# Row maxima of attention scores: from a relu of key differences to one maximum over two PSUM banks, with the keys in two groups of rows

## The chip, the cores and the metric

The kernel runs on one core of a Trainium2 chip. The metric is the device time of one execution in microseconds. The engines are TensorE (PE in the profile: matmuls; PEld: its weight loads), VectorE (DVE), ScalarE (ACT), GpSimd (POOL) and SyncE (SP), which here issues most DMAs. Each engine works through its own list of instructions in order. They meet at semaphores.

## The reference

An attention block with a gated bias by relative position, then a layer of eight experts. Shapes: 8 batches, 1024 tokens, 256 features, 16 heads of 16.

```python
q, k, v = split_heads(x @ Wq.T + bq), split_heads(x @ Wk.T + bk), split_heads(x @ Wv.T + bv)
pos_bias = transpose(rel_embed[buckets], (2, 0, 1))        # head, query, key
proj = (split_heads(x) @ gru_W.T + gru_b).reshape(B, H, N, 2, 4).sum(-1)
gate_a, gate_b = split(sigmoid(proj))
gate_out = gate_a * (gate_b * gru_const - 1.0) + 2.0
scores = einsum('bhid,bhjd->bhij', q, k) * scale + gate_out * pos_bias
attn = softmax(scores, axis=-1)
x = layernorm(x + (einsum('bhij,bhjd->bhid', attn, v) merged) @ Wo.T + bo)
# then: top 2 of 8 experts per token with a capacity, a fallback network for what spills
x = layernorm(x + experts(x))
```

## The kernel before, in words

The attention part works in units: one batch and two heads, 64 units in all. A unit has 16 steps. In the loop over `g`, step `s` of unit `u` stands for one block of 128 keys (`j`) and one half of the 1024 queries (`c`, 512 of them), for both heads. `scores` forms the transposed scores: two bf16 matmuls into the two banks of `sc`, of which there are two copies. `exps` adds the gated near bias (`gb`, made on GpSimd by `gate_biases`) on VectorE where the block has near keys, and takes the exponential of 128x1024 on ScalarE. On the odd steps `products` multiplies the exponentials with the values: four matmuls with 17 columns each, side by side, into `o_acc`. Queries and keys are held as three bf16 parts; `PRODUCTS` names the six pairs of parts that are stacked along the contraction, 16 rows each. Behind these 96 rows lie 24 rows for the far bias and two for the shift.

The exponential needs the largest score of each query first. That maximum is formed 21 steps (`LEAD`) ahead, one block of 128 queries and one head per step `m = g + LEAD`. The 1024 keys are split in two halves of each block of 128 keys. `max_first(m)` forms the scores of the difference between the first and the second half's keys (`KD`, in `ks_d`), with the difference of their biases, in the bank `pm1`; ScalarE's relu of it goes to `over`. `max_second(m)` forms the scores of the second half in the bank `pm0`, or on some even steps in the bank that the other streams share. `max_fold(m)` adds the two and takes the maximum over 512 columns in one VectorE instruction, since max(a, b) is b + relu(a - b). Each half takes two matmuls (`half_scores`): keys against queries (512 columns), and the near bias by a diagonal matrix of gates (`dgb`, from `diagonal` on GpSimd; 192 to 320 columns). Once a unit has its 16 maxima, `shift` transposes them and stores them as two rows of `QS`.

The order is written out by hand. Beside the steps run streams, Python generators that are moved on once per step: the next batch's projections (`prologue`, `halves`, `gating`), the last batch's output projection and expert choice (`epilogue`), and per unit `shift` and `divide`. Where a stream yields BANK, `streams.bank` lets it issue a matmul into the one shared bank (pool `ps_x`); where it yields HELD or SLOW, the read of that bank follows at the start of the next step, on ScalarE or VectorE (`streams.held`). Within a step the order is: `max_fold` of the maximum before, `held`, `scores`, `max_first`, `exps`, products, `bank`, `max_second`. If an even step's held read was SLOW (`behind`), `bank` follows `max_second`.

[...]four for `sc`, two for `pm0` and `pm1`, one shared, one for `o_acc`.

The operands of a unit are loaded by `load_unit` on SP's queue, two units ahead, at steps 3 (keys), 4 (differences) and 6 (queries), six or seven DMAs each, into `KS`, `KD` and `QS`. On the same queue are the bias windows (step 1 and 8), the gates (9 and 15), the sums of the exponentials and their reciprocals (steps 2 to 5, which `divide` needs at step 8), the outputs, and the streams' loads and stores.

After the attention the experts follow (from about 2600 us on); the change does not touch them.

Of the kernel before, what the change touches and what calls it, by code (L numbers as in the profile page):

```python
# [42 lines left out]
R_FAR, R_SHIFT, R_ALL = 6 * D, 6 * D + 24, 6 * D + 26  # L43
HP = 2
# [34 lines left out]
def tile_attention_moe(  # L79
# [73 lines left out]
    with ExitStack() as at:  # L153
# [16 lines left out]
        def bank(name):  # L170
            pool, tag = banks[0]
            banks.append(banks.pop(0))
            return pool.tile([P, CH], F32, tag=tag, name=name)
# [145 lines left out]
        for lo, hi in zip(cuts[:-1], cuts[1:]):  # L319
# [18 lines left out]
        nc.vector.tensor_tensor(  # L338
            strip16[:, 1, : STRIP - HALF], strip[:, : STRIP - HALF], strip[:, HALF:],
            ALU.subtract,  # L340
        )
# [17 lines left out]
        dd = [dram.tile([3, E, N // 2], BF16, name=f"dd{i}") for i in range(2)]  # L359
# [11 lines left out]
        QS = [cst.tile([R_ALL, HP, N], BF16, name=f"qs{i}") for i in range(3)]  # L371
        KS = [cst.tile([R_ALL, HP, N], BF16, name=f"ks{i}") for i in range(3)]
        KD = [cst.tile([R_SHIFT, HP, N // 2], BF16, name=f"ks_d{i}") for i in range(2)]
        pattern = once.tile([R_ALL, HP, N], F32, tag="oD", name="pattern")
        for h in range(HP):
            for part in range(3):
                r = R_FAR + part * NI
                nc.sync.dma_start(out=pattern[r : r + NI, h, :], in_=kcr[:NI, :])
            for r in range(R_SHIFT, R_ALL):
                nc.sync.dma_start(out=pattern[r : r + 1, h, :], in_=kcr[8:9, :])  # L380
        for t in KS:
            nc.gpsimd.tensor_copy(t[R_FAR:], pattern[R_FAR:])
        for t in KD:
            nc.gpsimd.memset(t[R_FAR:], 0.0)
# [26 lines left out]
        def first_part(n, parts, rest):  # L411
            after(n, lambda: nc.scalar.copy(parts[:, 0, :], rest))
            after(n + 1, lambda: nc.gpsimd.tensor_tensor(
                rest, rest, parts[:, 0, :], ALU.subtract
            ))

# [9 lines left out]


        def first_parts(parts, rest):
            nc.scalar.copy(parts[:, 0, :], rest)
            nc.gpsimd.tensor_tensor(rest, rest, parts[:, 0, :], ALU.subtract)  # L430

        def last_parts(parts, rest):
            nc.scalar.copy(parts[:, 1, :], rest)
            nc.gpsimd.tensor_tensor(parts[:, 2, :], rest, parts[:, 1, :], ALU.subtract)
# [174 lines left out]
        def halves(b, xT, m):  # L609
# [3 lines left out]
            for c in range(NCH):  # L613
                for w_sb, b_sb, dst in ((wk_sb, bk_sb, kd), (wq_sb, bq_sb, qd)):
# [14 lines left out]
                    pv = pq.rearrange("p (j a n) -> p j a n", a=2, n=HALF)  # L629
                    if dst is kd:  # L630

                        second = rt.tile([P, CH // 2], F32, tag="second", name="second")
                        sv = second.rearrange("p (j n) -> p j n", n=HALF)
                        nc.scalar.activation(
                            sv, pv[:, :, 1, :], AF.Identity, bias=bias, scale=1.0
                        )
# [9 lines left out]
                    if dst is kd:  # L646
                        dif = rt.tile([P, CH // 2], F32, tag="dif", name="dif")
                        dparts = work.tile(
                            [P, 3, CH // 2], BF16, tag="dparts", name="dparts"
                        )  # L650
                        nc.vector.scalar_tensor_tensor(
                            dif.rearrange("p (j n) -> p j n", n=HALF),
                            pv[:, :, 0, :], bias, sv, ALU.add, ALU.subtract,
                        )
                        first_part(1, dparts, dif)
                        second_part(3, dparts, dif)
                        after(5, lambda t=dparts, c=c: nc.sync.dma_start(
                            out=dd[b % 2][
                                :, ms, c * (CH // 2) : (c + 1) * (CH // 2)
                            ].rearrange("a r n -> r a n"),  # L660
                            in_=t,
                        ))
# [238 lines left out]
        def load_unit(u, which):  # L901

            b, hp = divmod(u, UB)
            assert batches[b].gated and batches[b].rows >= (hp + 1) * HP * D
            heads = slice(hp * HP * D, (hp + 1) * HP * D)
            if which == 2:
                nc.sync.dma_start(
                    out=QS[u % 3][R_FAR:R_SHIFT],
                    in_=fd[b % 2][:, :, hp * HP : (hp + 1) * HP, :].rearrange(
                        "a j h n -> (a j) h n"  # L910
                    ),
                )
            src, dst = ((kd, KS[u % 3]), (dd, KD[u % 2]), (qd, QS[u % 3]))[which]
            for r, parts in enumerate(PRODUCTS):
                nc.sync.dma_start(
                    out=dst[r * D : (r + 1) * D],
                    in_=src[b % 2][parts[which != 2], heads, :].rearrange(
                        "(h d) n -> d h n", d=D
                    ),
                )  # L920

# [89 lines left out]


        def half_scores(m, a, pm):
            u, n = divmod(m, STEPS)
            i, h = divmod(n, HP)
            me = units[u]
            lo, hi = max(i - NEAR, 0), min(i + NEAR + 1, NI)
            pm = pm.rearrange("p (j n) -> p j n", n=HALF)
            if a:
                keys = KD[u % 2][:, h, :].rearrange("p (j n) -> p j n", n=HALF)  # L1020
            else:
                keys = KS[u % 3][:R_SHIFT, h, :].rearrange("p (j n) -> p j n", n=P)[:, :, HALF:]
            nc.tensor.matmul(  # L1023
                pm, QS[u % 3][:R_SHIFT, h, i * P : (i + 1) * P], keys, start=True, stop=False
            )
            at = (h * 2 + a) * MWIN + (lo - i + NEAR) * P
            nc.tensor.matmul(  # L1027
                pm[:, lo:hi, :],
                dgb[m - h][:, h, :],
                me.biasb[:, at : at + (hi - lo) * P].rearrange("p (j n) -> p j n", n=P)[  # L1030
                    :, :, :HALF
                ],
                start=False,
                stop=True,
            )

        def max_first(m):

            u, n = divmod(m, STEPS)
            me = units[u]  # L1040
            ahead = m + 6
            if m == 0:
                for a in range(0, 6, 2):
                    dgb[a] = diagonal(0, a // 2)
            if ahead % 2 == 0 and ahead < UNITS * STEPS:
                dgb[ahead] = diagonal(ahead // STEPS, ahead % STEPS // HP)
            if n == 0:
                me.mh = rt.tile([P, HP, NI], F32, tag="mh", name=f"mh{u}", bufs=2)
            me.over = rt.tile([P, CH], F32, tag="over", name="over", bufs=2)
            pm = ps_m.tile([P, CH], F32, tag="pm1", name="pm1")  # L1050
            half_scores(m, 1, pm)
            nc.scalar.activation(me.over, pm, AF.Relu)  # L1052

        def max_second(m, common=False):

            pm = bank("pm") if common else ps_m.tile([P, CH], F32, tag="pm0", name="pm0")
            half_scores(m, 0, pm)
            units[m // STEPS].rest = pm

        def max_fold(m):  # L1060
            u, n = divmod(m, STEPS)
            i, h = divmod(n, HP)
            me = units[u]
            nc.vector.tensor_tensor_reduce(  # L1064
                out=me.over,
                in0=me.rest,
                in1=me.over,
                scale=1.0,
                scalar=-3.0e38,
                op0=ALU.add,  # L1070
                op1=ALU.max,
                accum_out=me.mh[:, h, i : i + 1],
            )

        def shift(u):
# [14 lines left out]
            def store():  # L1090
                for a in range(2):
                    nc.sync.dma_start(
                        out=QS[u % 3][R_SHIFT + a : R_SHIFT + a + 1].rearrange(
# [8 lines left out]
        def scores(u, j, c):  # L1102
            me = units[u]
            qs, ks = QS[u % 3], KS[u % 3]
# [159 lines left out]
        for u in range(2):  # L1264
            for which in range(3):
                load_unit(u, which)
            load_max_bias(u)
            clear_max_bias(u)
# [3 lines left out]
        for m in range(LEAD):  # L1272
# [6 lines left out]
            max_first(m)  # L1279
            streams.free()  # L1280
            streams.bank()
            max_second(m)
# [26 lines left out]
        for g in range(G + 12):  # L1309
# [4 lines left out]
            if g < G:  # L1314
# [7 lines left out]
                if u + 2 < UNITS:  # L1322
                    for which, at_ in enumerate((3, 4, 6)):
# [6 lines left out]
                if u + 1 < UNITS:  # L1330
                    if s == 8:
                        load_bias(u + 1)
# [6 lines left out]
            if g < G:  # L1339
                scores(u, j, c)  # L1340
                if m < G:
                    max_first(m)
# [16 lines left out]
            if m < G and g < G:  # L1359
                max_second(m, c == 0 and not behind and not streams.holder)  # L1360
# [10 lines left out]
        banks += [(ps_m, "pm0"), (ps_m, "pm1")]  # L1371
# [264 lines left out]
```

## Time and profile before

| | |
|---|---|
| median of 3 runs | 3706.02 us (3704.2 to 3713.74) |
| the profiled execution | 3705.5 us, of which its span 3703.8 us |
| granted TensorE clock over the span | 0.954 |
| exponentials of the attention loop | from 149.5 to 2523.6 us |
| busy from 1000 to 2000 us | PE 932.2, DVE 627.9, ACT 741.7, POOL 778.4 us |

In the rows of a profile, a group has its line, engine and operation, what it writes and reads, its count, then its busy time in us, the mean in ns, and how long its engine was idle just before it, with what ended most of that. In a timeline a row has its start in us, its duration in us, engine, line and operation, and a count where equal neighbours are merged. Matmuls overlap in the array, so the distance from one start to the next tells more than the duration.

### The profile page before, as it was taken

How to read it: one execution, taken by the hardware profiler on the slowest of the kernel's cores; microseconds unless marked ns; L12 is line 12 of the kernel's file. 1: busy time of each engine (PE TensorE's matmuls, PEld its weight loads, DVE VectorE, ACT ScalarE, POOL GpSimd, SP SyncE). 2: the span in 40 equal slices, each digit the busy share in tenths (PEclk: the TensorE clock that was granted, in tenths of full speed). 3: DMA queues.
4: the chain of work that ended last, by engine and by line, in shares of the span. 5: the costliest groups of instructions: out<-in, count | busy, mean ns of one | idle time of the engine just before them, and what ended most of it. 6: DMA issues, size and time to landing. Idle time of an engine off the chain costs nothing. (4 is left out here: it accounts for less than half of the span.)

```text
span 3703.8 us, 53431 instructions
## 1 busy us (share of the span) xinstructions
PE 3293.6 (89%) x16263; PEld 1663.7 (45%) x16263; DVE 1944.0 (52%) x5559; ACT 2045.0 (55%) x3084; POOL 2221.0 (60%) x2619
## 2 busy tenths in 40 slices
PE   4798898999899999999999999995299999999998
PEld 2242243334334334334333433332176667677776
DVE  2455566665756656665666576662033444344443
ACT  1576776777767777777777777772022222222222
POOL 2566666876886787787787688683333333333332
PEclk8899999999999999999999999996599999999999
DMA  5566666565543444444434444430322321332220
GB/s 133 153 167 192 167 172 183 173 195 181 179 140 110 144 135 122 134 136 122 139 123 141 133 123 128 129 111 15 107 70 74 90 87 54 92 94 94 71 89 22
DMA packets 380594, 455.71 MB, mean 123 GB/s; under 512 B 87653, under 2 KB 285410, under 8 KB 380282
## 3 DMA queue, kind: packets, MB, share of 16 engines
q1 hardware_dynamic: 338602, 388.06, 35.5%
q0 software_dynamic: 19296, 43.38, 4.1%
q10 hardware_dynamic: 22384, 20.58, 1.9%
q8 instruction: 138, 2.26, 0.3%
q14 instruction: 174, 1.43, 0.1%
HBM read 315.16 MB, written 140.54 MB: 123 GB/s over the span
## 5 line engine op out<-in xcount | busy, mean ns | idle before, releaser
L1129 ACT ACTIVATE pr<-sc 128x1024 f32<-128x1024 f32 x1024 | 1046.8, 1023 | 303.7 <-DVE sc L1122 297.9
L983 POOL TENSOR_TENSOR gb<-bias,gates 128x1024 f32<-128x1024 f32 (+2 forms) x512 | 1070.5, 2091 | 190.1 <-DMA gates<-gd 114.3
L1064 DVE CUSTOM_DVE_ANT_0 over<-pm,over 128x512 f32<-128x512 f32 x1024 | 704.3, 688 | 884.7 <-ACT over L1052 281.3
L1052 ACT ACTIVATE over<-pm 128x512 f32<-128x512 f32 x1024 | 609.3, 595 | 344.0 <-PE pm L1027 327.2
L1107 PE MATMUL sc<-qs,ks 122*128 122x512 bf16 x2048 | 625.1, 386 | 26.3 <-ACT pr L1129 18.5
L1122 DVE TENSOR_TENSOR sc<-sc,gb 128x640 f32<-128x640 f32 (+3 forms) x768 | 599.6, 781 | 46.6 <-POOL gb L983 21.0
L1027 PE MATMUL pm<-biasb,dgb 128*128 128x320 bf16 (+2 forms) x2048 | 581.7, 284 | 17.2 <-POOL dgb L996 17.2
L1137 PE MATMUL o_acc<-pr,v 128*17 128x512 f32 x4096 | 562.5, 621 | 0.3 <-ACT pr L1129 0.3
L1474 PE MATMUL ph<-xsT,w 128*128 128x512 f32 (+1 forms) x1440 | 487.6, 497 | 13.0 <-ACT xsT L1414 13.0
L1489 PE MATMUL py<-w,hT 128*128 128x256 f32 x2208 | 485.0, 379 | 5.9 <-DVE ys L1496 5.9
L1489 PEld LDWEIGHTS py<-w,hT 128*128 128x128 f32 x2208 | 419.2, 190 | 74.5 <-issue 10.5
L1023 PE MATMUL pm<-ks,qs 120*128 120x512 bf16 x1024 | 397.8, 388 | 57.3 <-DVE mh L1064 33.9
L1023 PE MATMUL pm<-ks_d,qs 120*128 120x512 bf16 x1024 | 397.1, 388 | 25.0 <-ACT over L1052 13.6
L1023 PEld LDWEIGHTS <-qs 120*128 120x128 bf16 x2048 | 208.9, 102 | 467.4 <-issue 303.4
L1481 ACT ACTIVATE hT<-ph,b_sb 128x512 f32<-128x512 f32 (+1 forms) x360 | 211.6, 588 | 287.3 <-PE ph L1474 286.3
L1474 PEld LDWEIGHTS ph<-xsT,w 128*128 128x128 f32 x1440 | 270.2, 190 | 212.7 <-issue 166.5
L1414 ACT COPY xsT<-pt 128x512 f32<-128x512 f32 (+1 forms) x90 | 39.5, 489 | 566.9 <-PE pt L1411 472.8
L143 POOL TENSOR_TENSOR rs<-rstd,neghalf 128x1 f32<-128x1 f32 x138 | 78.2, 566 | 442.2 <-DVE rstd L141 441.8
L1027 PEld LDWEIGHTS <-dgb 128*128 128x128 bf16 x2048 | 202.4, 99 | 301.6 <-issue 161.8
L996 POOL TENSOR_TENSOR dgb<-anti,grev 128x256 bf16<-128x256 f32 x512 | 314.2, 614 | 4.6
L1107 PEld LDWEIGHTS <-ks 122*128 122x128 bf16 x2048 | 199.8, 100 | 202.0 <-issue 52.3
L419 POOL TENSOR_TENSOR parts<-rest,parts 128x512 bf16<-128x512 f32 (+1 forms) x80 | 92.6, 1158 | 267.0 <-ACT parts L418 201.6
(184 smaller groups left out, 2929.7 us busy)
## 6 DMA issues: line engine op xcount, KB each, us to landing
gates<-gd SPq DMA_DIRECT2D x64, 832.0 KB
biasb<-stripb SPq DMA_DIRECT2D x128, 288.0 KB
gates<-gd SPq DMA_DIRECT2D x64, 576.0 KB
bias<-blocks SPq DMA_DIRECT2D x64, 512.0 KB
xd<-zero SPq DMA_DIRECT2D x51, 522.0 KB
ks<-kd SPq DMA_DIRECT2D x384, 64.0 KB
qs<-qd SPq DMA_DIRECT2D x384, 64.0 KB
yd<-zero SPq DMA_DIRECT2D x40, 512.0 KB
```

Source lines behind the costliest of these rows:

```text
L983: nc.gpsimd.tensor_tensor(gb_[:, :, off : off + hi - lo], me.bias[:, :, off : off + hi - lo], gates[:, :, lo - at : hi - at], ALU.mult,)
L996: nc.gpsimd.tensor_tensor(dg, anti.unsqueeze(1).to_broadcast([P, HP, P]), batches[b].grev[:, i, hp * HP : (hp + 1) * HP] .unsqueeze(2) .to ...
L1023: nc.tensor.matmul(pm, QS[u % 3][:R_SHIFT, h, i * P : (i + 1) * P], keys, start=True, stop=False)
L1027: nc.tensor.matmul(pm[:, lo:hi, :], dgb[m - h][:, h, :], me.biasb[:, at : at + (hi - lo) * P].rearrange("p (j n) -> p j n", n=P)[:, :, :HALF],
L1052: nc.scalar.activation(me.over, pm, AF.Relu)
L1064: nc.vector.tensor_tensor_reduce(out=me.over, in0=me.rest, in1=me.over, scale=1.0, scalar=-3.0e38, op0=ALU.add, op1=ALU.max, accum_out=me. ...
L1107: nc.tensor.matmul(me.sc[:, h, :], ks[:, h, j * P : (j + 1) * P], qs[:, h, c * CH : (c + 1) * CH], start=True, stop=True,)
L1122: nc.vector.tensor_tensor(sc[:, :, lo - c * CH : hi - c * CH], sc[:, :, lo - c * CH : hi - c * CH], me.gb[j][:, :, off : off + hi - lo], A ...
L1129: nc.scalar.activation(pr, sc, AF.Exp)
L1137: nc.tensor.matmul(o_acc[r : r + D + 1, :], batches[b].v[:, j, hp * HP + h, :], prs[c][:, h, :], start=(j == 0), stop=(j == NI - 1),)
L1474: nc.tensor.matmul(ph[:, :size], w1_sb[:, k, f * P : (f + 1) * P], xsT[:, k, :size], start=(k == 0), stop=(k == NK - 1),)
L1489: nc.tensor.matmul(py, hT[:, f, t * P : (t + 1) * P], w2_sb[:, f, :], start=(f == 0), stop=(f == NF - 1),)
```

## The change

Differences of keys, their parts and the store `dd` go, and so do the relu and `over`. The maxima get operands of their own, `QM` and `KM`, with three products of parts (`M_PRODUCTS`) instead of six: 48 rows, and 16 rows for two parts of the far bias, make 64. Rows 0 to 63 hold the second half of each block of keys, rows 64 to 127 the first half; the queries are there twice. `maxima(m)` takes the place of `max_first` and `max_second`: two key matmuls of 64 rows each, one on each group of rows, into the two banks of one tile `pm`, then the two bias matmuls. It stands where `max_second` stood. `max_fold` is one maximum over the 1024 columns of both banks. The second bias strip is now that of the first half itself, no longer a difference. `load_unit` has four parts; the operands of the scores are held for two units instead of three and loaded one unit ahead, those of the maxima two units ahead.

```diff
+M_PRODUCTS = PRODUCTS[:2] + PRODUCTS[3:4]
+M_FAR = 3 * D
...
-        QS = [cst.tile([R_ALL, HP, N], BF16, name=f"qs{i}") for i in range(3)]
-        KS = [cst.tile([R_ALL, HP, N], BF16, name=f"ks{i}") for i in range(3)]
-        KD = [cst.tile([R_SHIFT, HP, N // 2], BF16, name=f"ks_d{i}") for i in range(2)]
+        QS = [cst.tile([R_ALL, HP, N], BF16, name=f"qs{i}") for i in range(2)]
+        KS = [cst.tile([R_ALL, HP, N], BF16, name=f"ks{i}") for i in range(2)]
+
+        QM = [cst.tile([P, HP, N], BF16, name=f"qm{i}") for i in range(2)]
+        KM = [cst.tile([P, HP, N // 2], BF16, name=f"km{i}") for i in range(2)]
...
+            if which == 0:
+                for r, (_, part) in enumerate(PRODUCTS):
+                    rows(KS[u % 2], r * D, kd, part)
+            elif which == 1:
...
+                for r, (part, _) in enumerate(PRODUCTS):
+                    rows(QS[u % 2], r * D, qd, part)
+            elif which == 2:
+                for r, (_, part) in enumerate(M_PRODUCTS):
+                    for a, base in ((1, 0), (0, 64)):
+                        for h in range(HP):
+                            head = hp * HP + h
+                            nc.sync.dma_start(
+                                out=KM[u % 2][
+                                    base + r * D : base + (r + 1) * D, h, :
+                                ].rearrange("d (j n) -> d j n", n=HALF),
+                                in_=kd[b % 2][part, head * D : (head + 1) * D, :].rearrange(
+                                    "d (j a n) -> d j a n", a=2, n=HALF
+                                )[:, :, a, :],
+                            )
+            else:
+                for base in (0, 64):
+                    nc.sync.dma_start(
+                        out=QM[u % 2][base + M_FAR : base + 64],
+                        in_=far[:2].rearrange("a j h n -> (a j) h n"),
+                    )
+                    for r, (part, _) in enumerate(M_PRODUCTS):
+                        rows(QM[u % 2], base + r * D, qd, part)
...
-            me.over = rt.tile([P, CH], F32, tag="over", name="over", bufs=2)
-            pm = ps_m.tile([P, CH], F32, tag="pm1", name="pm1")
-            half_scores(m, 1, pm)
-            nc.scalar.activation(me.over, pm, AF.Relu)
...
-            pm = bank("pm") if common else ps_m.tile([P, CH], F32, tag="pm0", name="pm0")
-            half_scores(m, 0, pm)
-            units[m // STEPS].rest = pm
+            me.pm = ps_m.tile([P, 2, CH], F32, tag="pm", name="pm")
+            lo, hi = max(i - NEAR, 0), min(i + NEAR + 1, NI)
+            for a in range(2):
+                rows = slice(a * 64, a * 64 + 64)
+                nc.tensor.matmul(
+                    me.pm[:, a, :], QM[u % 2][rows, h, i * P : (i + 1) * P],
+                    KM[u % 2][rows, h, :], start=True, stop=False,
+                )
+            for a in range(2):
+                at = (h * 2 + a) * MWIN + (lo - i + NEAR) * P
+                nc.tensor.matmul(
+                    me.pm[:, a, :].rearrange("p (j n) -> p j n", n=HALF)[:, lo:hi, :],
+                    dgb[m - h][:, h, :],
...
-            nc.vector.tensor_tensor_reduce(
-                out=me.over,
-                in0=me.rest,
-                in1=me.over,
...
+            nc.vector.tensor_reduce(
+                me.mh[:, h, i : i + 1], me.pm.rearrange("p a n -> p (a n)"), AX.X, ALU.max
             )
...
-                    for which, at_ in enumerate((3, 4, 6)):
+                    for which, at_ in ((2, 4), (3, 7)):
                         if s == at_:
                             load_unit(u + 2, which)
...
+                    for which, at_ in ((0, 3), (1, 6)):
+                        if s == at_:
+                            load_unit(u + 1, which)
...
                 scores(u, j, c)
-                if m < G:
-                    max_first(m)
                 exps(u, j, c)
...
             if m < G and g < G:
-                max_second(m, c == 0 and not behind and not streams.holder)
+                maxima(m)
...
-        banks += [(ps_m, "pm0"), (ps_m, "pm1")]
+        banks += [(ps_s, "sc"), (ps_s, "sc")]
```

## The prediction, made before the changed kernel ran

> **What bounds the kernel now.** I read the page first: which engine is full, and in which part of the span.
>
> ```profile
> span 3703.8 us, 53431 instructions
> PE 3293.6 (89%) x16263; PEld 1663.7 (45%) x16263; DVE 1944.0 (52%) x5559; ACT 2045.0 (55%) x3084; POOL 2221.0 (60%) x2619
> L1064 DVE CUSTOM_DVE_ANT_0 over<-pm,over 128x512 f32<-128x512 f32 x1024 | 704.3, 688 | 884.7 <-ACT over L1052 281.3
> L1052 ACT ACTIVATE over<-pm 128x512 f32<-128x512 f32 x1024 | 609.3, 595 | 344.0 <-PE pm L1027 327.2
> L1122 DVE TENSOR_TENSOR sc<-sc,gb 128x640 f32<-128x640 f32 (+3 forms) x768 | 599.6, 781 | 46.6 <-POOL gb L983 21.0
> L1023 PE MATMUL pm<-ks,qs 120*128 120x512 bf16 x1024 | 397.8, 388 | 57.3 <-DVE mh L1064 33.9
> ```
>
> TensorE is the fullest, and the attention loop (exponentials from 149.5 to 2523.6 us) is where the change lies: 1024 steps, about 2.33 us each. VectorE (0.63 busy between 1000 and 2000 us) and ScalarE (0.74) have room. ScalarE's 609 us of relu are therefore no time of the kernel by themselves: between 1000 and 2000 us TensorE waits on the relu for 5.4 us only.
>
> A busy TensorE is not one at its peak, so I read its timeline next, for the distance from start to start. Two steps, an even one (from 1013.81) and an odd one (from 1015.16):
>
> ```profile
> 1013.81 0.60 PE L1107 MATMUL sc<-qs,ks 122*128 122x512 bf16 x2
> 1014.24 0.38 PE L1023 MATMUL pm<-ks_d,qs 120*128 120x512 bf16 x1
> 1014.46 0.25 PE L1027 MATMUL pm<-biasb,dgb 128*128 128x192 bf16 x1
> 1014.86 0.38 PE L1023 MATMUL pm<-ks,qs 120*128 120x512 bf16 x1
> 1015.07 0.25 PE L1027 MATMUL pm<-biasb,dgb 128*128 128x192 bf16 x1
> 1015.16 0.60 PE L1107 MATMUL sc<-qs,ks 122*128 122x512 bf16 x2
> 1015.59 0.38 PE L1023 MATMUL pm<-ks_d,qs 120*128 120x512 bf16 x1
> 1015.81 0.25 PE L1027 MATMUL pm<-biasb,dgb 128*128 128x192 bf16 x1
> 1015.99 1.05 PE L1137 MATMUL o_acc<-pr,v 128*17 128x512 f32 x8
> 1016.97 0.28 PE L1078 MATMUL pmr<-ident,mh 128*16 128x128 f32 x1
> 1017.08 0.38 PE L1023 MATMUL pm<-ks,qs 120*128 120x512 bf16 x1
> 1017.30 0.25 PE L1027 MATMUL pm<-biasb,dgb 128*128 128x192 bf16 x1
> 1017.39 0.60 PE L1107 MATMUL sc<-qs,ks 122*128 122x512 bf16 x2
> ```
>
> A 512-column bf16 matmul costs 0.215 us in a row of them, not 0.38; a bias matmul 0.09 to 0.14. I cut the PE rows between 1000 and 2000 us at every start of a scores pair: 429 steps, in four classes. Even steps without another stream's matmul: 141, mean 1.34 us. Odd ones without: 103, 2.49 (median 2.28; the products cost about 1.0). Even ones with stream work: 74, 2.90. Odd ones with: 111, 3.05. Weighted, 2.33 us. All but the first class are filled by TensorE's own work.
>
> Third, the stretch before the loop, where maxima run without scores. It shows what a chain "matmul, fold, same bank again" costs:
>
> ```profile
> 137.62 0.38 PE L1023 MATMUL pm<-ks,qs 120*128 120x512 bf16 x1 [0.57 <-DVE mh L1064]
> 137.83 0.27 PE L1027 MATMUL pm<-biasb,dgb 128*128 128x256 bf16 x1
> 138.25 0.69 DVE L1064 CUSTOM_DVE_ANT_0 over<-pm,over 128x512 f32<-128x512 f32 x1
> 139.00 0.38 PE L1023 MATMUL pm<-ks,qs 120*128 120x512 bf16 x1 [0.59 <-DVE mh L1064]
> ```
>
> 137.62 to 139.00 is 1.38 us: 0.21 keys, 0.27 bias, 0.15 to the fold, 0.69 fold, 0.06 back. In the main loop this chain is slack: the even step may take the shared bank for one half and the relu frees the other early.
>
> **The change, part by part.**
>
> *Fold.* One VectorE maximum over 1024 PSUM columns replaces 512 (0.69 us). The trace has no such instruction. Nearest row: the bias add L1122, also on PSUM, takes 293, 559, 827 and 1090 ns for 128, 384, 640 and 896 elements, that is 0.16 us plus 1.04 ns an element: 1.22 us for 1024. Bounds: 0.69 if it read two elements at a time, 1.35 if dearer by a tenth. I take 1.22, which is +0.53 on the chain (VectorE goes from about 1.48 to 1.92 us a step, not full by itself).
>
> *Single buffer.* Both halves are now one two-bank tile with one copy. The four matmuls of m+1 stand behind the fold of m, in TensorE's queue ahead of the next scores. So every step has a floor: keys together 0.22, switch 0.10, first bias 0.11, last bias with its end 0.27, to the fold 0.13, fold 1.22, back 0.06 = 2.11 us. During the 1.41 us of fold and hand-overs TensorE has only two scores (0.43) in an even step without stream work. Such steps go from 1.34 to 2.11, +0.77 us, and 32.9% of the 1003 loop steps that have maxima are such: 330, **+254 us**. Even steps whose only stream work is an expert count (13 of 429, mean 1.59, so 30) go to 2.11 too: **+15**. Before the loop the floor of 1.38 becomes 2.11 in some 13 of 20 folds: **+9**.
>
> *Row groups.* Of the two key matmuls one should disappear beside the other, -0.215 us, in steps that TensorE fills: 1003 - 330 - 30 = 643, which is -138 us. Against this stands a rule of the Trainium skill, "TensorEngine Tiling (Array Packing)", Key Properties: changing the tiling mode, not only the tile, drains the array. The row: the products use 17-column tiles, and at 1015.81 a bias matmul of 192 columns is through after 0.09 (as 1015.07 to 1015.16), yet the products start only after 0.18. A switch costs some 0.09 us; I use 0.10. Each step now switches twice more, into row groups and back. By the page's "up to 2x" alone the filled steps bring -138; with two switches of 0.10 they bring 643 x (-0.215 + 0.20) = **-10**. I take the second. That row groups run together no run here shows (column groups do: eight product records in 0.98 us); bounds of the overlap 0 and 0.215.
>
> *Relu gone.* ScalarE -0.595 us a step; it bounds nothing. TensorE's waits on relu and exponentials are 5.4 and 3.0 us in 1000: **-10** over the loop at most.
>
> *Held reads.* A stream's VectorE read stands behind the fold, so 0.53 later, and the one shared bank is free later. About 22 of 128 steps have such a read and a new bank matmul; 180 steps at 0 to 0.53, say 0.25: **+45**. This wait also holds the maxima behind that matmul.
>
> *SP's queue.* A unit's loads go from 19 DMAs to 33: keys 6, queries 7, maxima's keys 12, maxima's queries 8. At 0.46 us each (six in 2.75) that is +6.4 us of SP a unit. Twelve instead of six stand before the four reciprocals, which so land 2.8 later; TensorE's matmul on them waited 24.7 us in 1000 already. The maxima's queries come last: from the sums at step 2 on, 2.4 + 2.9 + 5.5 + 2.4 + 3.3 + 3.7 and some 2 to land = 22 us, and they are needed at step 11, 9.4 steps later: 21.9 us at 2.33 a step, 24.6 at 2.62. Longer steps cover it, except with a batch's gate stores (16 more DMAs) in between. Bounds 0 and 150; I take **+15**. The 128-byte runs (1536 a unit) at the present mean of 62 ns a packet are 6 us of 16 engines a unit, under the free half of them.
>
> *At nothing:* differences of keys (12 subtractions of 675 ns in 1000 us on POOL, 12 casts and copies on ScalarE), covered because neither engine bounds; uncovered they would be worth -40 us in all. *Moved:* the loads for the scores come one unit ahead instead of two, at steps 3 and 6 of the unit before; they are needed 10 steps (23 us) later, which covers them. The diagonal matrices on POOL are issued behind the exponentials of a step instead of ahead of them, six maxima before their use. TensorE loads as many weights as before. Setup: a few memsets and copies on POOL, 0 to +5. Tail and experts unchanged.
>
> Sum: 254 + 15 + 9 - 10 - 10 + 45 + 15 = +318 us. On the profiled execution's 3705.5 (span 3703.8; median of the runs 3706.0) this gives 4023; I say **4025 us**, a loop of about 2.65 us a step.
>
> **The rivals.**
>
> *Faster (0.05).* TensorE's savings win. It needs a cheap fold: a step's floor is 0.89 plus the fold. Without any switch cost the filled steps give 138 us, and 330 even steps may lose 0.42 each: the fold would have to end within 0.87 us. At 0.69 and no switches the floor is 1.48, the loss 46, and the time about 3706 - 138 + 46 = 3615. For it: the filled classes are two thirds of the steps. Against: the slope of L1122.
>
> *Cheap chain (0.08).* The fold as computed, but switches cost nothing: floor 2.01, 330 x 0.67 = 221, -138, with the small terms +40: about 3830.
>
> *No overlap (0.12).* The row groups run one after the other: +0.215 in all 1003 steps, 4025 + 216 = 4240. The change would then not do what it says.
>
> *SP late (0.10).* Some 2.4 us of stall per unit at step 11: 64 x 2.4 = 155, 4180.
>
> **How the numbers follow.** The chain as summed: 0.65, own range 3920 to 4130. The 80% range reaches to half of the cheap chain and to the late queue: 3860 to 4200; it leaves out most of "no overlap", "faster" and some of "cheap chain". Differences under 0.3% (11 us), about what a measurement of this kernel can tell, get 0.01; slower 0.94.
>
> **What would show it.** Right: on the page, PE's busy share in the loop falls; the maximum takes about 1.22 us; the key matmuls now wait on mh for several hundred us; even steps without stream work take 2.1 us; the first key matmul of a pair and the second start within 0.02 us; 0.1 us gaps around them. Wrong: a maximum under 0.9 us, even steps under 1.7 us, key matmuls 0.2 us apart, or waits of the key matmuls on DMA (qm) that add up to more than 100 us.

## The result, and the profile after

The changed kernel takes 4201.86 us (median of four, 4201.02 to 4204.63), the kernel before 3708.02: a ratio of 1.1331 (95% interval 1.1314 to 1.1348), or 494 us more. Forecast were 319 us more, with 4200 as the end of the range. The chain of matmul and fold was there, in the size computed; of two terms beside it, one was about nine times too small and one about twice.

From the page of the profile after, the rows that answer to those of before:

```profile
span 4202.8 us, 50578 instructions
PE 3347.5 (80%) x16263; PEld 1585.0 (38%) x16263; DVE 2444.5 (58%) x4503; ACT 1495.8 (36%) x1964; POOL 2184.7 (52%) x2558
...
L1051 DVE TENSOR_REDUCE mh<-pm 128x1 f32<-128x1024 f32 x1024 | 1249.1, 1220 | 904.9 <-PE pm L1037 894.4
L1109 ACT ACTIVATE pr<-sc 128x1024 f32<-128x1024 f32 x1024 | 1033.6, 1022 | 1594.1 <-DVE sc L1102 1556.3
...
L1031 PE MATMUL pm<-km,qm 64*128 64x512 bf16 x2048 | 432.1, 403 | 383.5 <-DVE mh L1051 368.7
...
L1157 PE MATMUL pb<-recs,sel 4*128 4x512 f32 x128 | 107.4, 931 | 177.9 <-DMA recs<-sums 163.5
```

The maximum takes 1220 ns, as the slope of the bias adds had said. The key matmuls wait 369 us on it (before: 34). Neither VectorE nor TensorE is full: they wait for each other, VectorE 894 us for the maxima's last matmul, TensorE 369 us for the fold. The last row is the one that was not forecast at its size. TensorE's waits for the reciprocals (us in total, times, longest), before and after:

```profile
PE pb L1177 <- DMA recs<-sums: 74.6, 29, 8.3
```

```profile
PE pb L1157 <- DMA recs<-sums: 163.5, 46, 8.3
```

The mean duration of that matmul rises from 666 to 931 ns.

The timeline of the changed kernel, one even step without stream work:

```profile
1506.32 0.60 PE L1087 MATMUL sc<-qs,ks 122*128 122x512 bf16 x2
1506.53 1.23 DVE L1051 TENSOR_REDUCE mh<-pm 128x1 f32<-128x1024 f32 x1
1507.80 0.39 PE L1031 MATMUL pm<-km,qm 64*128 64x512 bf16 x2 [0.88 <-DVE mh L1051]
1508.13 0.45 PE L1037 MATMUL pm<-biasb,dgb 128*128 128x320 bf16 x2
1508.41 0.60 PE L1087 MATMUL sc<-qs,ks 122*128 122x512 bf16 x2
```

From scores to scores 2.09 us, where an even step took 1.35: scores, fold, maxima, one after the other, with TensorE idle for 0.88. The two key matmuls run together (they start 0.005 us apart in the median of all pairs, and take 0.39 us as a pair, the duration of one). The first bias matmul starts 0.33 us after the first of them: 0.22, the distance of one 512-column matmul before, for both, and about 0.1 that is put down to leaving the row groups.

Cut at every start of a scores pair, as in the prediction, but over the whole loop (from 150 us on), the steps give this table. A class holds mean us, and the sum in us; "reciprocals" are the steps with the matmul that divides by the sums (step 8 of a unit, or soon after), and "early" and "reads" are two experiments below.

| class (count) | before | after | early | early, reads |
|---|---|---|---|---|
| even, no stream work (350 to 352) | 1.33, 464 | 2.05, 722 | 2.06, 726 | 2.04, 717 |
| even, reciprocals (50) | 3.85, 193 | 6.49, 324 | 2.35, 117 | 2.38, 119 |
| even, other streams (111) | 2.54, 282 | 2.91, 323 | 2.94, 327 | 2.83, 314 |
| odd, no stream work (251) | 2.47, 620 | 2.36, 594 | 2.53, 634 | 2.49, 626 |
| odd, stream work (246) | 3.09, 759 | 3.41, 840 | 3.43, 845 | 3.21, 789 |
| odd, reciprocals (13) | 4.10, 53 | 3.98, 52 | 3.97, 52 | 3.15, 41 |

From before to after the first row is +258 us; the second +131, for 50 steps; the third and the fifth, with other streams' work, +41 and +81; the fourth -26.

The second row is SP's queue, on which the reciprocals are loaded. Its timeline, first before, then after, from a unit's sums to its reciprocals:

```profile
1064.65 2.44 SPq L1154 DMA_DIRECT2D sums<-osb  x4
1067.19 2.86 SPq L915 DMA_DIRECT2D ks<-kd  x6
1070.09 2.76 SPq L915 DMA_DIRECT2D ks_d<-dd  x6
1072.94 2.44 SPq L1164 DMA_DIRECT2D recs<-sums  x4
```

```profile
1510.96 2.44 SPq L1134 DMA_DIRECT2D sums<-osb  x4
1513.51 2.86 SPq L887 DMA_DIRECT2D ks<-kd  x6
1516.41 7.64 SPq L907 DMA_DIRECT2D km<-kd  x12
1524.14 2.44 SPq L1144 DMA_DIRECT2D recs<-sums  x4
```

Twelve loads of the maxima's keys take 7.6 us of SP, 0.64 each; the six of the differences took 0.46 each. The reciprocals start 13.2 us after the sums, not 8.3. What that does on TensorE, in another unit of the changed kernel:

```profile
1069.50 0.60 PE L1087 MATMUL sc<-qs,ks 122*128 122x512 bf16 x2
1073.17 2.04 PE L1157 MATMUL pb<-recs,sel 4*128 4x512 f32 x2 [3.07 <-DMA recs<-sums]
...
1075.14 0.61 PE L1031 MATMUL pm<-km,qm 64*128 64x512 bf16 x2
1075.68 0.61 PE L1037 MATMUL pm<-biasb,dgb 128*128 128x256 bf16 x2
1076.09 1.06 PE L1087 MATMUL sc<-qs,ks 122*128 122x512 bf16 x2
```

A wait of 3.07 us, and behind it the array runs at half its rate: 1.06 us for a scores pair that took 0.60. The trace has a granted clock of 0.50 from 1072.9 to 1079.7 us, and 1.00 around that. Over the loop (160 to 2970 us) the granted clock is 0.92, before 0.97.

### The profile page after: what moved, and what is told of

Same layout as the page of the kernel before. It is cut to its first block, busy times and chain, and to the rows that moved or that the text cites. A ratio compares the mean times of both kernels' runs of the same rounds, so it can differ in the third digit from the quotient of the medians.

```text
span 4202.8 us, 50578 instructions
## 1 busy us (share of the span) xinstructions
PE 3347.5 (80%) x16263; PEld 1585.0 (38%) x16263; DVE 2444.5 (58%) x4503; ACT 1495.8 (36%) x1964; POOL 2184.7 (52%) x2558
## 5 line engine op out<-in xcount | busy, mean ns | idle before, releaser
L1051 DVE TENSOR_REDUCE mh<-pm 128x1 f32<-128x1024 f32 x1024 | 1249.1, 1220 | 904.9 <-PE pm L1037 894.4
L1109 ACT ACTIVATE pr<-sc 128x1024 f32<-128x1024 f32 x1024 | 1033.6, 1022 | 1594.1 <-DVE sc L1102 1556.3
L1031 PE MATMUL pm<-km,qm 64*128 64x512 bf16 x2048 | 432.1, 403 | 383.5 <-DVE mh L1051 368.7
L1087 PE MATMUL sc<-qs,ks 122*128 122x512 bf16 x2048 | 650.7, 400 | 11.9 <-ACT pr L1109 6.8
L1117 PE MATMUL o_acc<-pr,v 128*17 128x512 f32 x4096 | 596.5, 656 | 0.3 <-ACT pr L1109 0.3
L1031 PEld LDWEIGHTS <-qm 64*128 64x128 bf16 x2048 | 145.4, 93 | 928.2 <-issue 913.0
L1037 PE MATMUL pm<-biasb,dgb 128*128 128x320 bf16 (+2 forms) x2048 | 432.5, 295 | 23.6 <-POOL dgb L998 23.6
L1157 PE MATMUL pb<-recs,sel 4*128 4x512 f32 x128 | 107.4, 931 | 177.9 <-DMA recs<-sums 163.5
L1489 POOL DMA_INDIRECT out_dram<-o,dst_i x138 | 144.9, 1050 | 160.2 <-DVE o L148 66.9
L1037 PEld LDWEIGHTS <-dgb 128*128 128x128 bf16 x2048 | 117.6, 98 | 275.6 <-issue 236.8
```

Source lines behind the costliest of these rows:

```text
L1031: nc.tensor.matmul(me.pm[:, a, :], QM[u % 2][rows, h, i * P : (i + 1) * P], KM[u % 2][rows, h, :], start=True, stop=False,)
L1037: nc.tensor.matmul(me.pm[:, a, :].rearrange("p (j n) -> p j n", n=HALF)[:, lo:hi, :], dgb[m - h][:, h, :], me.biasb[:, at : at + (hi - lo) ...
L1051: nc.vector.tensor_reduce(me.mh[:, h, i : i + 1], me.pm.rearrange("p a n -> p (a n)"), AX.X, ALU.max)
L1087: nc.tensor.matmul(me.sc[:, h, :], ks[:, h, j * P : (j + 1) * P], qs[:, h, c * CH : (c + 1) * CH], start=True, stop=True,)
L1109: nc.scalar.activation(pr, sc, AF.Exp)
L1117: nc.tensor.matmul(o_acc[r : r + D + 1, :], batches[b].v[:, j, hp * HP + h, :], prs[c][:, h, :], start=(j == 0), stop=(j == NI - 1),)
```

## Experiments

The ratios are to the kernel before on the same chip; the changed kernel stands at 1.1331.

**The keys' loads behind the reciprocals.**

```diff
-                    for which, at_ in ((2, 4), (3, 7)):
+                    for which, at_ in ((2, 6), (3, 7)):
```

> The changed kernel with one number changed: the twelve loads of the maxima's keys are issued at step 6 instead of step 4, and so behind the four loads of the reciprocals. Nothing else moves: maxima's queries still come last. Theory A (TensorE stalls at the reciprocals' matmul because twelve loads of 0.64 us stand ahead of the reciprocals on SP's queue; the clock drops after each stall): the reciprocals are issued about 7.7 us earlier in a unit, waits of that matmul on its data fall from 230 us to under 40, even steps with it from 6.5 us to about 3, granted clock over the loop from 0.92 to 0.96 or more; time about 4000 (3960 to 4040). Rival B (the 128-byte runs load the DMA engines, and the order does not matter): within 40 us of 4202. Rival C (the stall only moves to step 11, since the maxima's queries are as late as before): waits on qm of over 100 us, time 4120 or more.

4242.19 us, 1.1387 (1.136 to 1.1414). Theory A fell as a forecast of the time, and its first half came true: even steps with the reciprocals' matmul fall from 6.49 to 2.32 us. The time went to the next use, as rival C had it: odd steps with other streams' work grow from 840 us of sum to 1041. TensorE's waits by what they wait for:

```profile
PE pm L1031 <- DVE mh L1051: 360.4, 429, 1.6
PE pm L1031 <- DMA qm<-qd: 161.6, 82, 4.8
```

In the changed kernel the maxima's key matmuls wait 4 us for these loads of `qm`; here 162. The queries' loads come last in SP's order in both kernels, but in the changed one the stall at step 8 had given them the time. As long as all these loads stand between step 2 and step 11, their order only chooses who waits.

**The maxima's loads a unit early**, at steps 13 and 14, when SP has little to do.

```diff
-                    for which, at_ in ((2, 4), (3, 7)):
-                        if s == at_:
-                            load_unit(u + 2, which)
+                    if g == 0:
+                        load_unit(2, 2)
+                        load_unit(2, 3)
...
+                if u + 3 < UNITS:
+                    for which, at_ in ((2, 13), (3, 14)):
+                        if s == at_:
+                            load_unit(u + 3, which)
```

> The changed kernel with all twenty loads for the maxima (keys and queries) issued at steps 13 and 14, a whole unit's lead, where SP otherwise idles. Theory A: as with the keys behind the reciprocals, about 4000, and no wait on qm left; if it is 20 us or more faster than that kernel, the queries' lateness at step 11 was worth that. Rival B (traffic, not order): within 40 us of 4202.

4059.17 us, 1.0903 (1.0873 to 1.0934). The same loads with the same bytes, and 0.043 of the time, 159 us, is gone: order, not traffic. The granted clock in the loop is 0.95. It is 59 us over the forecast of 4000: the scores now wait 38 us for the rows that `shift` stores (5 in the changed kernel), and the late reads (below) are still there.

**Without row groups.** Each half's keys get 128 rows, zeros in the other half's.

```diff
-        KM = [cst.tile([P, HP, N // 2], BF16, name=f"km{i}") for i in range(2)]
+        KM = [cst.tile([P, HP, 2, N // 2], BF16, name=f"km{i}") for i in range(2)]
...
-                rows = slice(a * 64, a * 64 + 64)
...
-                    me.pm[:, a, :], QM[u % 2][rows, h, i * P : (i + 1) * P],
-                    KM[u % 2][rows, h, :], start=True, stop=False,
+                    me.pm[:, a, :], QM[u % 2][:, h, i * P : (i + 1) * P],
+                    KM[u % 2][:, h, a, :], start=True, stop=False,
```

> The changed kernel without row groups: each half's keys fill 128 rows, with zeros in the 64 rows of the other half, so the two key matmuls run one after the other and no tiling mode is switched. The loads are the same. It prices the two groups of rows: the row says that from the first key matmul to the first bias matmul takes 0.32 us with them (0.22 and a switch); without them it should take 0.43, and the switch in front of the keys goes too. Predicted term (two switches cost what the overlap brings): within 20 us of 4202. Rival (the overlap pays, as odd steps with a median of 2.12 against 2.28 say): slower by 0.1 us in about 640 steps plus 0.1 in the 330 chain-bound ones, 60 to 100 us.

4227.13 us, 1.135 (1.1316 to 1.1383): not to be told from 1.1331. But the stall levels such differences, so it was run again with early loads.

> The kernel with the maxima's loads issued early, without row groups (each half's keys fill 128 rows, zeros in the other half's rows). Its partner is the early loads' 4059 (1.0903 of the kernel before). It prices the two groups of rows with the stall at the reciprocals out of the way. If the prediction's term holds (overlap 0.215 given back by two switches): within 20 us of the partner. If the overlap pays 0.1 us a step, as the class medians with the stall say (2.17 and 2.23 against 2.08 and 2.12): 60 to 100 us slower, 4120 to 4160.

4054.6 us, 1.0913 (1.0885 to 1.0942), against 1.0903 with row groups: nothing. Yet the maxima's matmuls take longer in each step, here in an even one:

```profile
1503.23 0.59 PE L1034 MATMUL pm<-km,qm 128*128 128x512 bf16 x2 [0.54 <-DVE mh L1054]
1503.66 0.43 PE L1040 MATMUL pm<-biasb,dgb 128*128 128x320 bf16 x2
1503.93 0.60 PE L1090 MATMUL sc<-qs,ks 122*128 122x512 bf16 x2
```

From the first key matmul to the first bias matmul it takes 0.43 us instead of 0.33, and the medians of even and odd steps without stream work are 2.18 and 2.23 instead of 2.08 and 2.12. What gives it back was not isolated: odd steps with and without stream work together take 36 us less than with row groups, and the granted clock in the loop is 0.98 here and 0.95 with them, which goes that way.

**Half the fold**: the maximum over the first bank only, so that half of the keys are left out of it.

```diff
-                me.mh[:, h, i : i + 1], me.pm.rearrange("p a n -> p (a n)"), AX.X, ALU.max
+                me.mh[:, h, i : i + 1], me.pm[:, 0, :], AX.X, ALU.max
```

> The changed kernel, whose maximum reads only the first of the two banks (512 columns): the maximum leaves out half of the keys; all four matmuls stay. It prices the length of the fold. Theory (chain matmul, fold, same tile again): the fold falls from 1.22 to 0.69 us, the floor of a step from 2.08 to 1.55; even steps without stream work go to about 1.55, 377 of them save 0.53 each, 200 us, and the held reads of streams come 0.53 earlier, 40 to 90 us more; waits of the key matmuls on the fold fall to about a quarter. The stall at the reciprocals stays or grows, since steps get shorter. Time 3950 to 4030. Rival (TensorE's work or the transfers bound, the fold is hidden): 4150 or more.

4093.22 us, 1.1015 (1.0983 to 1.1047), short of the forecast. Even steps without stream work fall to a median of 1.55 as computed, but the steps with the reciprocals grow from 6.49 to 8.41: shorter steps reach the late reciprocals sooner. With early loads:

> The kernel with the maxima's loads issued early, and a maximum over the first bank only (the maximum leaves out half of the keys; all matmuls stay). The stall at the reciprocals is out of the way, so the chain is priced free of it. Theory (chain): against the early loads' 4059, some 365 even steps save 0.55 each and the fold's lateness in stream steps goes: -200 to -280 us, 3780 to 3860. Rival (TensorE waits elsewhere for the same time, as with the half fold alone, where 109 of some 200 us came through): -110 or less.

3896.53 us, 1.0499 (1.0471 to 1.0527): 0.040, 150 us under the early loads, below the 200 forecast. The even steps without stream work gave 189 us of sum back (726 to 537), 0.54 us each. Part of it went into the scores' wait for the shift rows, whose stores stand behind the early loads on SP: it grew from 38 to 133 us.

**One bank, one copy against two.** Half of the maxima's matmuls are left out, and the fold reads one bank twice, so that it keeps its length. The edit is that with two copies; its control has `bufs=1`.

```diff
-            me.pm = ps_m.tile([P, 2, CH], F32, tag="pm", name="pm")
+            me.pm = ps_m.tile([P, 1, CH], F32, tag="pm", name="pm", bufs=2)
...
-                me.mh[:, h, i : i + 1], me.pm.rearrange("p a n -> p (a n)"), AX.X, ALU.max
+                me.mh[:, h, i : i + 1], me.pm.to_broadcast([P, 2, CH]), AX.XY, ALU.max
```

> The changed kernel with the maximum of the second half of the keys only, in one bank, one copy; the VectorE maximum reads that bank twice over, so that it stays at 1024 columns and 1.22 us. Half of the maxima's matmuls are left out. It is the control for the same with two copies. Chain theory: floor 0.27 + 0.22 + 0.13 + 1.22 + 0.06 = about 1.9 us, still what even steps without stream work take; time about 4100.

> As the kernel with one bank and one copy, but two copies of that bank: the same instructions, only the wait of a key matmul is on the fold before the last. It prices the single copy by itself. Chain theory: even steps without stream work fall from 1.9 to 1.3 to 1.5 us, waits of the key matmuls on the fold nearly vanish, and the time falls by 150 us or more against the single copy. Rival (VectorE itself is full: maximum 1.22, bias add 0.58 and streams 0.3 a step): falls by less than 60 us, and VectorE is busy over 0.9.

4197.34 us with one copy (1.1295), 4147.99 with two (1.1163, 1.1084 to 1.1241). Even steps without stream work fall from a median of 1.93 to 1.00, and the steps with the reciprocals rise from 6.90 to 8.94. Again with early loads:

> The kernel with the maxima's loads issued early, with the maximum of the second half of the keys only (half of the maxima's matmuls left out), in two copies of one bank, the VectorE maximum of 1024 columns reading that bank twice. Its control is the same with one copy (next). Chain theory: 180 us or more faster than with one copy, since only the copy differs: even steps without stream work 1.0 to 1.3 against 1.9. Rival (VectorE is full): within 60 us of it.

> The control of the kernel before in this list: one bank, one copy, loads early, half of the maxima's matmuls left out. Chain theory: even steps without stream work 1.9 us; time 4000 to 4050, little under the early loads' 4059, since the matmuls left out are in the chain's shadow or 0.2 us each in steps that TensorE fills.

4040.33 us with one copy (1.0887, 1.0859 to 1.0915), 4003.69 with two (1.0791, 1.0738 to 1.0844): 36 us, where the chain theory said 180. The wait for the fold does nearly go. TensorE's waits with one copy, then with two:

```profile
PE pm L1031 <- DVE mh L1051: 410.1, 446, 5.3
...
PE sc L1087 <- DMA qs<-row: 25.0, 10, 4.2
...
PE sc L1087 <- ACT pr L1109: 11.1, 16, 1.4
```

```profile
PE sc L1087 <- ACT pr L1109: 106.2, 178, 5.2
PE sc L1087 <- DMA qs<-row: 86.4, 34, 6.9
...
PE pm L1031 <- DVE mh L1051: 62.3, 33, 4.7
```

With two copies TensorE runs ahead until it meets the exponentials, which wait for the bias adds; these stand behind the folds on VectorE. Even steps without stream work lose 176 us of sum (688 to 512), and the other classes take 163 of it back: odd steps without stream work grow from 2.53 to 2.73 us. The exponentials' wait for the adds is the same with one copy and with two (493 and 488 us between 1000 and 2000 us), as it would be if VectorE's own order set the pace: a fold of 1.22 us per step in front of the adds. That is likely, not shown: 61 of the 163 us are SP's, in the wait for the shift rows, and the granted clock in the loop falls from 0.91 to 0.88. VectorE is busy 0.74 of the time, less than the rival said.

**The held reads ahead of the fold**, on odd steps, with early loads.

```diff
+            if c == 1:
+                streams.held()
             if g < G and m <= G:
                 max_fold(m - 1)
-            streams.held()
+            if c == 0:
+                streams.held()
```

> The kernel with the maxima's loads issued early, in which on odd steps the streams' held read stands ahead of the fold on VectorE instead of behind it. It prices the held reads: the shared bank comes free 1.2 us earlier, while products and scores fill TensorE. Theory (held reads late: odd steps with stream work 3.43 against 3.09 in the kernel before, 246 of them): these steps fall to 3.1 to 3.2, time -50 to -85 us, 3975 to 4010. Rival (their excess is the clock after stalls, or the chain): within 20 us of 4059, or slower since the fold comes later.

3962.24 us, 1.0671 (1.0645 to 1.0697): 0.023, 86 us. An odd step of the changed kernel shows the wait that this removes:

```profile
1066.68 1.05 PE L1117 MATMUL o_acc<-pr,v 128*17 128x512 f32 x8
1068.39 0.63 PE L706 MATMUL px<-ident,xt 128*128 128x128 f32 x4 [0.66 <-DVE v L501]
```

The transposes of a stream (`px`) need the shared bank, and the read that frees it stands behind the 1.22 us fold. Odd steps with these transposes take 2.73 us before, 3.27 after, and 2.67 with the read in front.

**The early loads behind the shift rows**, at steps 14 and 15, on top of that.

```diff
-                    for which, at_ in ((2, 13), (3, 14)):
+                    for which, at_ in ((2, 14), (3, 15)):
```

> The kernel with early loads and reads ahead of the fold on odd steps (3962), with those loads at steps 14 and 15 instead of 13 and 14, so that they follow the two small stores of the shift rows on SP instead of preceding them. In that kernel the scores wait 42 us on these rows. Theory (the stall is whatever stands last in SP's order before a use): the wait on the rows goes, 30 to 50 us faster, 3910 to 3935. Rival (the stall moves to the next use again, as it did with the keys behind the reciprocals): within 15 us of 3962.

4143.27 us, 1.1151 (1.1123 to 1.1179): 178 us worse, outside both theories. The wait on the rows is gone. But SP stands in order: it now waits for the rows to be ready before it issues any of the twenty loads, and the gates' load of step 15 comes behind all of them. SP's timeline with the loads at 13 and 14, then here:

```profile
1515.47 8.88 SPq L907 DMA_DIRECT2D km<-kd  x12
1524.45 1.17 SPq L1072 DMA_DIRECT2D qs<-row  x2
...
1529.61 0.38 SPq L967 DMA_DIRECT2D gates<-gd  x1
```

```profile
1514.92 2.42 SPq L1171 DMA_DIRECT2D oD<-osb  x4
1523.26 1.15 SPq L1072 DMA_DIRECT2D qs<-row  x2
1524.50 7.66 SPq L907 DMA_DIRECT2D km<-kd  x12
...
1536.14 0.38 SPq L967 DMA_DIRECT2D gates<-gd  x1
```

From the rows to the gates it is 12.9 us instead of 5.2, and SP has stood still for 5.9 us before the rows. GpSimd's waits on gates, first with the loads at 13 and 14, then here:

```profile
POOL gb L985 <- DMA gates<-gd: 197.8, 51, 12.8
```

```profile
POOL gb L985 <- DMA gates<-gd: 436.0, 59, 14.4
```

Late gates make late biases, the adds wait for them, and the fold waits behind the adds: TensorE's wait for the fold grows from 411 to 519 us.

**The two orders in the kernel before.** First its differences' loads behind the reciprocals:

```diff
-                    for which, at_ in enumerate((3, 4, 6)):
+                    for which, at_ in ((0, 3), (1, 6), (2, 7)):
```

> The kernel before, with the six loads of the key differences moved from step 4 to step 6 and the queries' from 6 to 7, so that the reciprocals are issued 2.8 us earlier. Theory A: the matmul on the reciprocals waited 75 us there, 2.8 us earlier takes most of it: 3706 minus 50 to 80, and the clock rises a little from 0.954. Rival B: no change.

3691.39 us, 0.9916 (0.9895 to 0.9938): 31 us, where 50 to 80 were expected. Even steps with the reciprocals fall from 193 us of sum to 124, and here too a part comes back as other waits of TensorE (for exponentials 44 us instead of 18, for the shift rows 16 instead of 7). With the held reads ahead of the fold on odd steps too:

> The kernel before with both orders that paid: the loads of the differences behind the reciprocals (0.9916 of before), and on odd steps the streams' held VectorE read ahead of the fold. There the fold is 0.69 us, not 1.22, so the reads are less late: 10 to 40 us more, 0.981 to 0.989. Rival: the fold comes later and the maxima with it, no gain or a loss.

3670.65 us, 0.9878 (0.9853 to 0.9902). The two intervals touch, so that the reads' share there is not settled. With the differences' loads at step 14 for three units ahead and the queries' at step 6:

> As the last, but the differences' loads a unit ahead at step 14, behind the shift rows, and the queries' load back at step 6. The waits on queries (18 us) should go: 10 to 20 us less than the last. Rival: the loads at step 14 delay the sums at step 2, no gain.

3636.29 us, 0.9786 (0.9762 to 0.9809): 34 us under the last, more than the 10 to 20 expected, and the fastest of all, 2.1% under the kernel before, without the change.

## Why the prediction missed, step by step

*Held: the fold and the floor.* 1.22 us was forecast and 1220 ns measured; the floor of an even step 2.11, measured 2.08 (median); the sum +254, measured +258. Half the fold, with early loads, gives 189 us of it back, so the fold's length is the cause. Two parts of the floor were off and cancel, which is luck; in the row at 1508.13 the two bias matmuls take 0.45 us to their end (0.38 forecast) and the fold follows 0.03 later (0.13 forecast). The 0.15 "to the fold" before the loop was not a hand-over, since VectorE was still busy with another instruction:

```profile
137.48 0.75 DVE L639 SCALAR_TENSOR_TENSOR rest<-pq,bq_sb,parts 128x512 f32<-128x512 f32 x1
```

What was not right is the name, "single buffer". With half of the maxima's matmuls left out, two copies bring 36 us; half the length brings 150. The floor was computed from a chain that has the fold in it. Behind that chain there seems to stand another, fold and add on VectorE, hardly shorter; that it is this one and not SP or the clock is not shown.

*Failed: SP's queue, +15.* The steps with the reciprocals show that this term was too small: +131 us from before to after. The early loads gain 159 in all, more than the change had added, for they also take away most of what the kernel before waited there. Three things were wrong in that step. The price of a load: 0.46 us was taken from the other loads, the maxima's keys take 0.64. The deadline: the text compared the maxima's queries at step 11 with a mean step of 2.62 us. The reciprocals come first, at step 8, and the six steps ahead of them take 13.4 us in the median, where SP needs 13.2 us from the sums to the start of the reciprocals' loads. And the clock: a stall of 3 us is followed by matmuls at a granted 0.50. The text had the 2.8 us of delay and the 25 us already waited, and then costed only the later deadline. As a rival, "SP late", it stood at 155 us, at the wrong step and with a chance of 0.10.

*Failed: the held reads, +45.* Steps with other streams' work take 122 us more in the table, where this term and the +15 for the expert counts make 60. With early loads TensorE waits some 50 us in the loop for VectorE's reads of the shared bank, in the kernel before some 12; with the reads in front 1 is left, and 86 us are gained. The same move in the kernel before gains some 14, not settled, so not all of the 86 is the change's. Of a read that comes later, more was waited for than the half that the text took: single waits are about as long as the delay of 0.5 us (0.66 at 1068.39).

*Row groups, -10.* The total held: no difference with or without. The working is not confirmed. The pair does run together, and of the two switches of 0.10 us only the one out of the row groups is seen; the pair saves 0.1 us in every step, and something of about that size takes it away. The rule of the Trainium skill, "TensorEngine Tiling (Array Packing)", Key Properties, that a change of tiling mode drains the array, agrees with the 0.1 us between the keys' streaming and the first bias matmul; the "up to 2x" of its section Theoretical Speedup is true of the pair (0.39 us) and of nothing else here.

*The rivals.* In "faster" the fold's limit without switches is 0.97 us, not 0.87, since that floor has no switch in it. At 1.22 us this changes nothing.

*The sum.* 249 us are left with early loads and reads in front (1.0671); 249, 86 and 159 are the 494. The prediction's other terms give 254 + 15 + 9 - 10 - 10 = 258, but that is no confirmation: the kernel before gains from the same kinds of order, too. Against its fastest run (0.9786) the changed kernel with both orders is 0.0885, 328 us, slower. So, as far as the two sets of orders can be compared, 166 of the 494 us go with SP's queue and the reads, where the prediction had 60, and 328 with the rest, where it had 258. Even steps without stream work make 251 of the 328, and the scores' waits for the shift rows 40 (42 against 1); the other 37 were not followed up.

## What to carry to other kernels

When DMAs are added to a queue that works in program order, go through every use that stands behind them, first the next one. Take the steps at the length that they have there and not at their mean, and expect that a reordering may only move the wait to the next use. Look for idle time of the queue a whole round earlier, and compare a repaired kernel with an equally repaired one.

An instruction that gets longer on an in-order engine costs more than its length where others stand behind it: here adds, held reads and the matmuls of the next step. Ask for each what waits for it, and whether it can stand in front.

## What was not expected of the hardware

A load of the maxima's keys (16 rows in 128 runs of 128 bytes, 16 KB) occupies SP's queue for 0.64 us from start to start, one of the scores' keys (16 rows in 32 runs of 2 KB, 64 KB) for 0.47; these are medians of the changed kernel. So the time does not follow the bytes. The number of runs may be the reason; no run varies it alone.

TensorE's clock: in the changed kernel TensorE waits 46 times for the reciprocals, up to 8 us, and the granted clock in the loop is 0.92 instead of 0.97; the early loads bring it to 0.95. The kernels that leave out half of the maxima's matmuls run at 0.91 and 0.88 with early loads. So part of what a saved matmul gives may be taken back by the clock; why the clock is lower there was not isolated.
